# Attention in a decoder: transposes in half-array tiles, exponentials taken after the transpose, sums from the values' matmul

## The chip, the cores and the metric

The kernel runs on one core of a Trainium2 chip. The metric is the device time of one execution in microseconds, the median of several runs. The engines are TensorE (PE; its weight loads are shown apart as PEld), VectorE (DVE), ScalarE (ACT), GpSimd (POOL) and SyncE (SP), which issues the DMAs.

## The reference

A decoder of two layers on `x` of 8 batches, 256 tokens and 256 features, in float32, each sublayer followed by a residual addition and a layer norm:

```python
x = ln(x + gated_recurrence(x))                  # z = sigmoid, h by a scan over the tokens
x = ln(x + xattn0(x, ctx, bias, mask))           # 16 heads of 16, additive bias per batch
x = ln(x + ternary_ffn(ln'(x)))                  # activations quantised by one global maximum
x = ln(x + self_attn(x, rel_k, rel_v))           # distances clipped to 20 in scores and values
x = ln(x + xattn1(ctx, x, mask))
x = ln(x + gated_ffn(x))                         # 256 -> 768 -> 256, weights of int8 range

attn = softmax(q @ k.T / 4 + bias, axis=-1)      # 256 x 256 for each batch and head
out  = (attn @ v) @ Wo.T + bo
```

So there are 3 attentions x 8 batches = 24 items, each with 16 heads of 256x256 scores.

## The kernel before

**Order of the work.** Every piece of work is a Python generator that asks a planner (`Order`, L87) for an engine, a cost, the times at which its operands are ready, and buffers. The planner keeps a clock for each engine, takes the operation that can start first (among those within 0.1 us, the most urgent), and emits its instructions. So the order on each engine is fixed at build time by these costs; `either` and `copy` (L288) let it choose DVE or ACT for a copy. Tiles come from `Slots`, of which a task holds one until it drops it. There are 8 PSUM banks of 128x512 float32 (`banks`); `pv_left` lets two items at a time hold a bank for their values.

**Stages.** `recurrence` for 8 batches; `item_x0` (layer 0's cross-attention) for 8 batches; a barrier, since the quantisation needs a maximum over all batches; `quantised`; then `item_s1` (self-attention) and `item_x1` (layer 1's cross-attention) mixed by places set by hand (`S1_AT`, `X1_AT`); at the end `gated`, the last feed-forward. `keys_values` computes layer 1's keys and values into DRAM as filler. The self-attention sends its distance scores through DRAM scratch to skew them (`to_scratch`, `to_bands`, `tails_task`).

**One item.** `project_q`, `project_k` and `project_v` are each 8 TensorE passes of 256 columns. The 16 heads go as 4 quads of 4 heads (`quad`, L897):

- scores: 4 heads in 4 row tiles of 32 rows, each head into a bank of its own (L914);
- DVE takes each bank, adds the bias and writes the negated scores `sn` and their minimum `nm` (L942, a fused operation, 128x256 twice for each head);
- `head` (L953): ACT takes the exponential with `nm` as bias, and its sum over the keys (L958, 128x256 twice), into the quad's `p`;
- PE transposes the head's 256x256 by four 128x128 transposes into a bank (`transposed`, L503), and ACT or DVE copies it out to `pts` (L291, L292);
- `values` (L983): 4 heads in 4 column tiles of 32, into one bank that the item keeps through all four quads (L998).

`scales` (L1018) takes the reciprocals of the sums, POOL spreads them over the features (L1028), PE transposes them, they are copied to `oT`; `attend_out` multiplies the values by them (L1050), projects, adds the residual and norms. `norm` (L528) asks POOL for the root (L544, L549) and DVE for two scaled passes (L554). `distances` (L1454) adds the self-attention's distance values into the item's bank (L1483).

Weights for queries and keys come padded from DRAM (2 KB rows, L399) and POOL packs them (L477).

## Time and profile before

| | |
|---|---|
| median of 3 runs | 819.88 us (814.5 to 820.38) |
| span of the profiled execution, first to last instruction | 807.4 us |
| the median stands above this span by | 12.5 us |
| instructions | 21273 |
| granted TensorE clock, mean | 0.998 |
| DMA | 77.67 MB in 177681 packets, mean 96 GB/s |

The page gives the span of the profiled execution; what lies around it is read from the runs' median.

The engines' busy time in forty equal slices (tenths of a slice), with the DMA engines' mean busy share:

```profile
PE   7999999999999999997999999999999999999995
DVE  3998989989787698887799999898898999989986
ACT  2339999899988457786597799999999899845942
POOL 4440321122111044233333304313242323110010
DMA  5736352100100449889978706743656333100001
```

A slice is 20.2 us. The start and the last slice are thin; the dip of ACT and DVE near slices 13 to 15 is the barrier between the layers, and DMA is dense in slices 15 to 24, where the self-attention starts. A group's row gives its count, the busy time (overlaps counted once), the mean time of one instruction, and the idle time of its engine just before; neighbouring instructions overlap by some tenths of a microsecond, so the interval from start to start is shorter than the mean.

### The profile page before, as it was taken

The numbers are of one execution on the slowest core, as the hardware profiler recorded it, in microseconds if no ns is written. First come the engines' busy times: TensorE is split into PE (matmuls) and PEld (weight loads), VectorE is DVE, ScalarE is ACT, GpSimd is POOL, SyncE is SP. The second block draws the span as 40 slices with busy tenths as digits, with TensorE's granted clock in tenths as the row PEclk, the third lists the DMA queues.
The fourth block names the chain that finished last, engine by engine and source line by source line (L and its number), as shares of the span: only waits on it lengthen the run. The fifth ranks groups of instructions, "written<-read, shape, count | busy, mean of one in ns | idle before, by whom it ended". The sixth has DMA issues, their size and how long they took to land. (4 is left out here: it accounts for less than half of the span.)

```text
span 807.4 us, 21273 instructions
## 1 busy us (share of the span) xinstructions
PE 774.9 (96%) x7175; PEld 597.3 (74%) x7175; DVE 703.4 (87%) x2461; ACT 629.7 (78%) x2036; POOL 210.4 (26%) x398
## 2 busy tenths in 40 slices
PE   7999999999999999997999999999999999999995
PEld 6787777777766787665767677767776767899885
DVE  3998989989787698887799999898898999989986
ACT  2339999899988457786597799999999899845942
POOL 4440321122111044233333304313242323110010
PEclk9999999999999999999999999999999999999999
DMA  5736352100100449889978706743656333100001
GB/s 183 221 120 97 26 74 50 40 15 28 40 14 15 144 116 220 173 166 154 192 159 170 137 7 145 166 87 89 121 120 139 85 72 114 40 15 16 26 14 39
DMA packets 177681, 77.67 MB, mean 96 GB/s; under 512 B 155046, under 2 KB 171430, under 8 KB 177574
## 3 DMA queue, kind: packets, MB, share of 16 engines
q1 hardware_dynamic: 177574, 76.32, 43.4%
q8 instruction: 57, 0.93, 0.5%
q14 instruction: 50, 0.41, 0.2%
HBM read 41.66 MB, written 34.64 MB: 94 GB/s over the span
## 5 line engine op out<-in xcount | busy, mean ns | idle before, releaser
L958 ACT ACTIVATE p<-sn,nm 128x256 f32<-128x256 f32 x768 | 381.5, 510 | 14.1 <-DVE nm L942 8.2
L503 PE MATMUL pt<-ident,p 128*128 128x128 f32 x1536 | 208.4, 278 | 4.3 <-ACT p L958 1.8
L503 PEld LDWEIGHTS pt<-ident,p 128*128 128x128 f32 x1536 | 169.4, 141 | 50.5 <-ACT p L958 30.2
L292 ACT COPY pts<-pt 128x512 f32<-128x512 f32 x277 | 148.3, 591 | 34.5 <-PE pt L503 29.6
L958 ACT ACTIVATION_READ_ACCUMULATOR p<-sn,nm 128x1 f32 x768 | 154.4, 201 | 0.0
L914 PE MATMUL s<-k,q 32*128 32x256 f32 (+2 forms) x1792 | 118.6, 370 | 0.5 <-ACT pts L292 0.3
L998 PE MATMUL pv<-pts,v 128*32 128x256 f32 x1536 | 104.0, 385 | 0.0
L942 DVE CUSTOM_DVE_ANT_0 sn<-s,bias 128x256 f32<-128x256 f32 x256 | 93.1, 419 | 10.0 <-ACT p L958 5.8
L942 DVE CUSTOM_DVE_ANT_0 sn<-s,hide 128x256 f32<-128x256 f32 x256 | 92.8, 418 | 8.2 <-PE s L914 5.3
L942 DVE CUSTOM_DVE_ANT_0 sn<-s,band 128x256 f32<-128x256 f32 x256 | 92.3, 418 | 8.6 <-PE s L914 3.5
L914 PEld LDWEIGHTS s<-k,q 32*128 32x128 f32 x1792 | 77.2, 185 | 30.1 <-issue 20.1
L291 DVE COPY pts<-pt 128x512 f32<-128x512 f32 x107 | 71.1, 683 | 6.7 <-PE pt L503 6.3
L998 PEld LDWEIGHTS pv<-pts,v 128*32 128x32 f32 x1536 | 41.7, 109 | 41.5 <-issue 19.1
L942 DVE DVE_READ_ACCUMULATOR2_ANT nm<- 128x1 f32 x768 | 63.0, 82 | 0.0
L1028 POOL COPY rsw<-rsum 128x512 f32<-128x512 f32 x24 | 14.6, 610 | 157.4 <-DVE rsum L1022 139.0
L520 PE MATMUL pso<-wvo,oT 128*128 128x256 f32 x192 | 46.3, 385 | 0.4 <-ACT pts L292 0.4
L520 PEld LDWEIGHTS pso<-wvo,oT 128*128 128x128 f32 x192 | 35.1, 190 | 7.8 <-issue 1.3
L1354 POOL COPY band<-ends 64x256 f32<-64x256 f32 x64 | 21.5, 360 | 70.8 <-DVE nm L942 70.8
L1426 DVE TENSOR_REDUCE acc<-tail 128x8 f32<-128x864 f32 x32 | 33.4, 1045 | 5.3 <-POOL tail L1415 5.3
L1327 POOL COPY w<-w 128x504 f32<-128x504 f32 x32 | 19.6, 613 | 68.8 <-DVE w L291 40.7
L1709 ACT ACTIVATE sg<-fg 128x512 f32<-128x512 f32 x24 | 14.3, 599 | 21.7 <-PE fg L1698 21.6
L520 PE MATMUL psv<-wvo,ctxT 128*128 128x256 f32 x128 | 30.8, 384 | 0.0
(197 smaller groups left out, 1321.3 us busy)
## 6 DMA issues: line engine op xcount, KB each, us to landing
sk<-w SPq DMA_DIRECT2D x32, 416.0 KB
band<-sk SPq DMA_DIRECT2D x64, 104.0 KB
pb<-p SPq DMA_DIRECT2D x64, 104.0 KB
band<-sk SPq DMA_DIRECT2D x64, 84.0 KB
pb<-p SPq DMA_DIRECT2D x64, 84.0 KB
acc<-pb SPq DMA_DIRECT2D x32, 156.0 KB
ctxT<-in_ctxT SPq DMA_DIRECT2D x16, 256.0 KB
wpad<-in_qk_w SPq DMA_DIRECT2D x6, 512.0 KB
```

The lines of the kernel that those rows point to most:

```text
L291: ("DVE", on_dve(n), lambda: nc.vector.tensor_copy(dst, src)),
L292: ("ACT", on_act(n), lambda: nc.scalar.copy(dst, src)),
L503: nc.tensor.transpose(ps[:, c, t * P : (t + 1) * P], src[:, t, c * P : (c + 1) * P], ident)
L520: nc.tensor.matmul(ps[:, t, :], srcT[:, c, t * P : (t + 1) * P], w[:, c, :], start=(c == 0), stop=(c == KC - 1),)
L914: nc.tensor.matmul(ps[j].tile[:, t, first : first + w], it.q.tile[32 * j : 32 * j + 32, c, t * P : (t + 1) * P], k[32 * j : 32 * j + 32, c ...
L942: nc.vector.tensor_tensor_reduce(out=s.tile[:, t, :], in0=ps[j].tile[:, t, :], in1=tile[:, t, :], scale=-1.0, scalar=3e38, op0=ALU.add, op ...
L958: nc.scalar.activation(p.tile[:, j, q, :], s.tile[:, q, :], AF.Exp, bias=nm[:, q : q + 1], scale=-1.0, accum_out=it.sum_of(q, h),)
L998: nc.tensor.matmul(it.pv.tile[32 * j : 32 * j + 32, c, :], it.v.tile[:, k, head_of(n, j), :], pts.tile[:, k, :], start=(k == 0 and i == 0 ...
L1028: lambda: nc.gpsimd.tensor_copy(wide.tile.rearrange("p t (h d) -> p t h d", d=DH), rs.unsqueeze(3).to_broadcast([P, NQ, H, DH]),),
L1327: nc.gpsimd.tensor_copy(w.tile[:, :, NR:], w.tile[:, :, NR - 1 : NR].to_broadcast([P, HH, PBW - NR]))
L1354: nc.gpsimd.tensor_copy(band.tile[0:BLK, :, t, lo:hi], it.ends[c][0:BLK, t, i:HH:2].unsqueeze(2).to_broadcast([BLK, 4, hi - lo]),)
L1426: lambda: nc.vector.tensor_reduce(acc[:, c, :, own, 1], tail.tile, AX.X, ALU.add),
```

## The change

- Transposes (`transposed_pair`): two heads at a time, each 128x128 cut in two halves of 64 rows that are transposed in two row tiles of the array, into two banks; `pts` holds pairs (5 of them instead of 8 single ones).
- Cross-attention (`item.whole`, 16 of 24 items): no exponential before the transpose. DVE writes the negated, biased scores into `p`, POOL computes `nm - p` in place (`head_whole`), PE transposes, and ACT's exponential reads the transposed banks and writes `pts`. The sums come from the values' matmul: columns 16 to 31 of each head's values are ones. DVE's 32x32 block transposes, reciprocals and multiplications (`divided`) make `oT`. `scales` stays for the self-attention alone.
- Self-attention (8 items) keeps the exponential before the transpose; it has values tiles of its own, and its distances go into a bank of their own and are added by DVE.
- Values: a bank for each quad (cross) or two quads (self) instead of one for the item.
- The fourth bank of each quad's scores is copied to `p` by ACT, and DVE's minimum then reads `p`. The `sn` buffers are gone; the quad's `p` is taken together with the score banks.
- Query and key weights are loaded packed, in pieces of 64 bytes; POOL's packing is gone.
- Fewer buffers: one `oT`; one `y`, one `v`, one `mask8` and one `hide` (bfloat16) for layer 1's cross-attention; the mask of layer 0 shares `neg`. The planner may skip a starved task when nothing else can go, has other costs for changes of tile shape, and gives 0.5 us for a pair's transposes.

```diff
+    def transposed_pair(ps, srcs):
+        for j, src in enumerate(srcs):
+            for c in range(2):
+                for t in range(2):
+                    for g in range(2):
+                        own = slice(g * BLK, (g + 1) * BLK)
+                        nc.tensor.transpose(
+                            ps[g][:, 4 * j + 2 * c + t, :],
+                            src[own, t, c * P : (c + 1) * P],
+                            ident[own, own],
+                            tile_position=(g * BLK, 0),
+                        )
...
+    def minimum(it, n, j, p, ps, t_s, tile, t_b, t_bias, left, times):
+        own = p.tile[:, j]
...
+        if j != 3:
+            t = yield from do("DVE", 0.7, [t], lambda: least(ps.tile))
+            ps.drop(t)
+        else:
+            t = yield from do("ACT", on_act(512), [t_s], move)
+            ps.drop(t)
+            t = yield from do("DVE", 0.7, [t, t_b, t_bias], lambda: least(own))
...
+    def head_whole(it, n, j, p, nm, t, left):
+        def emit():
+            for q in range(NQ):
+                own, m = p.tile[:, j, q, :], nm[:, q : q + 1]
+                nc.gpsimd.tensor_scalar(own, own, -1.0, m, ALU.mult, ALU.add)
+        t = yield from do("POOL", 0.9, [t], emit)
...
+    def pair(it, n, m, done):
+        ps = [Held(banks, f"pt{it.name}_{n}_{m}_{g}") for g in range(2)]
...
+        for g in range(2):
+            dst = halves_of(pts.tile)[g]
+            if it.whole:
+                t = yield from do(
+                    "ACT", on_act(512), [t_p, pts.at],
+                    lambda: nc.scalar.activation(dst, parts(g), AF.Exp),
+                )
+            else:
+                t = yield from copy([t_p, pts.at], dst, parts(g))
...
-            it.token = yield from get(pv_left, "")
-            it.pv = Held(banks, f"pv{it.name}")
+        if it.whole or i == 0:
+            pv = it.pv[n] = Held(banks, f"pv{it.name}_{n}")
+        else:
+            pv = it.pv[n - 1]
...
+    def divided(it, c, i, pv, t):
...
+            lambda: nc.vector.transpose(
+                u[:, :, i : i + 2, :].rearrange("p n a d -> p n (a d)"),
+                pv.tile[:, 0, :].rearrange("p (n e) -> p n e", e=32),
+            ),
...
+            nc.vector.reciprocal(rec, u[:, :, i + 1, 0])
+            nc.vector.tensor_tensor(
+                u[:, :, i, :], u[:, :, i, :], rec.unsqueeze(2).to_broadcast([P, n, DH]), ALU.mult
+            )
...
+            lambda: nc.vector.transpose(
+                it.oT.tile.rearrange("p c (n e) -> p (c n) e", e=32),
+                it.u.tile[:, :, 0:2, :].rearrange("p n a d -> p n (a d)"),
+            ),
...
-    mask8_bufs = slots(work, "mask8", 2, [P, NQ, S], U8)
-    hide_bufs = slots(work, "hide", 2, [P, NQ, S])
+    mask8_bufs = slots(work, "mask8", 1, [P, NQ, S], U8)
+    hide_bufs = slots(work, "hide", 1, [P, NQ, S], BF16)
```

## The prediction

> **What bounds the kernel now.** First I read the engines' busy time on the profile's page, then the same in five stretches cut where the stages change.

> ```profile
> PE 774.9 (96%) x7175; PEld 597.3 (74%) x7175; DVE 703.4 (87%) x2461; ACT 629.7 (78%) x2036; POOL 210.4 (26%) x398
> ```
> ```profile
> 0.00:94.00 94.00, 87.92 (x593) 71.58 (x594) 75.81 (x241) 50.79 (x155) 32.00 (x56) 1.00 0.57 139
> 94.00:271.00 177.00, 173.59 (x1562) 129.19 (x1560) 150.29 (x584) 153.80 (x522) 31.31 (x43) 1.00 0.16 38
> 271.00:400.00 129.00, 119.97 (x1029) 89.28 (x1030) 109.50 (x349) 88.23 (x258) 44.54 (x104) 1.00 0.84 169
> 400.00:692.00 292.00, 288.30 (x3067) 212.20 (x3068) 268.80 (x1033) 271.47 (x933) 88.97 (x172) 1.00 0.55 116
> 692.00:807.40 115.40, 105.09 (x931) 95.00 (x929) 99.00 (x258) 65.37 (x173) 13.62 (x25) 0.99 0.06 19
> ```

> Columns: stretch, length, busy us of PE, weight loads, DVE, ACT, POOL; then granted clock, DMA share, GB/s. From 94 to 271 us layer 0's cross-attention runs alone (seven items, 25.3 us each); 271 to 400 is the barrier and the filling of layer 1, with DMA at 0.84; 400 to 692 is self- and cross-attention mixed; then the last feed-forward. PE's busy time has modelled ends, so I price PE by the starts in its timeline:

> ```profile
> 548.98 1.19 PE L914 MATMUL s<-k,q 32*128 32x148 f32 x24
> 550.10 2.00 PE L520 MATMUL pso<-wvo,oT 128*128 128x256 f32 x8
> 551.93 1.89 PE L509 MATMUL psq<-xT_l1a,wqk 128*128 128x256 f32 x8
> 553.65 2.35 PE L503 MATMUL pt<-ident,p 128*128 128x128 f32 x20
> 555.93 0.50 PE L914 MATMUL s<-k,q 32*128 32x256 f32 x4
> ```

> A projection (8 of 256 columns) takes 551.93 to 553.65: 1.72 us, 0.215 each. A 128x128 transpose takes 2.28/20 = 0.114 (0.109 inside a burst). Four tiles of 32 rows run at once: 24 score matmuls in 1.12 us; a whole quad's 16 take about 0.86, its 16 values matmuls 0.88. One layer 0 item therefore costs PE 4 x (0.86 + 1.75 + 0.88) for its quads, 4 x 1.73 for projections, 2 x 0.44 for other transposes, some 22 with tile changes: 22 of 25.3 us. The other engines' prices:

> ```profile
> L958 ACT ACTIVATE p<-sn,nm 128x256 f32<-128x256 f32 x768 | 381.5, 510 | 14.1 <-DVE nm L942 8.2
> L503 PE MATMUL pt<-ident,p 128*128 128x128 f32 x1536 | 208.4, 278 | 4.3 <-ACT p L958 1.8
> L292 ACT COPY pts<-pt 128x512 f32<-128x512 f32 x277 | 148.3, 591 | 34.5 <-PE pt L503 29.6
> L942 DVE CUSTOM_DVE_ANT_0 sn<-s,bias 128x256 f32<-128x256 f32 x256 | 93.1, 419 | 10.0 <-ACT p L958 5.8
> L291 DVE COPY pts<-pt 128x512 f32<-128x512 f32 x107 | 71.1, 683 | 6.7 <-PE pt L503 6.3
> ```

> From start to start (neighbours overlap) an exponential with its sum takes 0.49 us, ACT's copy 0.477, a DVE minimum 0.345, DVE's copy 0.60. ACT then spends 32 x 0.49 + 11.5 x 0.477 = 21.2 us on an item, DVE about 20.6 (11.0 on minima). So three engines are within 10% of each other and each loses some 12% to the others. No chain through one engine explains the time; relieving one leaves the next.

> **The change part by part.**

> *Transposes in row tiles.* 1536 of 128 columns become 3072 of 64 columns, in two halves of the array. By 0.109/128 a 64-column one streams 0.055. If the halves run together, a pair of heads costs 8 x 0.055 = 0.44, against 0.87: 0.43 x 192 pairs = 83 us off PE. The gain's lower bound is zero: 16 x 0.055 = 0.88. I take 0.46, nearest the score rows, where four 32-row tiles overlap; with about 70 more changes of tile shape (410 against 343 in program order) at 0.09 (a score-to-transpose step is 0.305 against 0.216), PE falls by some 73 us, 3.3 per item.

> [...] The score rows above, 24 loads of 32x128 inside 1.12 us, show that loads into different rows overlap.

> *Late exponentials.* In 16 of 24 items the 512 row exponentials of 0.49 go; 256 of 128x512 from PSUM replace both them and the copies out. Their price lies between ACT's copy (0.477) and twice a 256-wide one (0.98); a 512-wide tanh from PSUM starts 0.488 before its successor, the same shape, so 0.49. Per item ACT goes from 21.2 to 16 x 0.49 + 4 x 0.477 (the fourth score bank) = 9.8, some 11 with copies moved there; over the kernel about 614 to 465.

> *POOL's multiply-and-add.* 512 of 128x256. The row of 128x512 (mean 748, 0.617 when undisturbed) bounds one above by 0.62; 128x2 at 0.19 bounds it below. 64x256 copies start 0.34 apart; I take 0.36 to 0.40, between 512 and 2 elements. An item's POOL work goes from 4.3 to about 16 us, less than the pace, but 200 us in all, and the norms' root, the bias addition and the residual addition now queue behind it.

> *Sums out of the values, division on DVE.* Per x item: four transposes of 128x256 (0.33 as other 256-wide rows, up to 0.60 if at half rate), four reciprocals (0.15) and multiplications of 128 elements (0.2), one transpose of 128x512 (0.6): 3.3 us. Gone: 4.5 copies of 0.60, the scale's copy, reciprocal and product (1.3), a few projections' outputs that the planner now gives to ACT (0.5). Net about -1.1 per item. Self-attention keeps its exponentials and gains two additions and copies of 256: about level. Over the kernel DVE loses some 27 of 676 us. That is little: DVE is the engine left.

> *What POOL takes from DVE.* DVE's normalising pass, SBUF to SBUF, is normally 0.41 us:

> ```profile
> L554 DVE TENSOR_SCALAR xn<-xb,mv_l0x,rs_l0x x16: 401/408/1358, 93.7 to 270.7; 128x256 f32<-128x256 f32 x16
> ```

> Its one 1358 lies beside a 1.27 us POOL addition; a two-SBUF-input g<-g,h went from 0.68 to 0.93 beside POOL, and an a<-z on POOL to 1657. Minima on PSUM are 0.42 either way. The fourth minimum now reads two SBUF operands (192 of them), so with the norms and divisions about 17 DVE instructions an item can meet POOL. Free: 0. Each waiting for a whole POOL instruction: 17 x 0.36 = 6 us. POOL is busy 50 to 70%, and half an instruction is left on average: 17 x 0.6 x 0.18 = 1.8 per item.

> [...]

> *Buffers.* Values no longer keep two of eight banks for an item's length, and the fourth bank leaves early: worth the few per cent that PE loses on waits, at most. A quad's scores now also wait for one of three p buffers, each held over minima, POOL and transposes, some 9 us: one every 3 us, against a pace of 5.7, so nothing. Against the gain, layer 1's cross items have one mask, one values and one output buffer instead of two. A drain between them costs 0 (feed-forward work covers it) to 6 us (a quad's chain); if the cover is gone, twice in the last stretch. I put 2 us there.

> *Queues.* SP issues the six weight loads as twelve, 0.47 us each, and no unpacking on POOL (0.75 x 6) follows. 64-byte pieces: the nearest 80-byte packets take 12 ns, so 4096/16 x 12 = 3.1 us per weight against 256/16 x 84 = 1.3: +11 us of transfer in a start where recurrences on DVE (24 of 25 us busy from 25 to 50) cover it; bare, the two first weights would cost 3.6. Masks share a buffer with what they become; the wait is behind an addition 20 us earlier.

> *Sum by stretch.* 0 to 94: 0. 94 to 271: PE 18.5 to 19, DVE 19.5 + 1.8 = 21.3; with the other two relieved, DVE can run at 0.93, its share in the best stretch (47.9 of 50 busy from 400 to 450, less overlap): 22.9 an item, 7 x 2.4 = -17. 271 to 400: DMA holds, -4. 400 to 692: DVE 268.8, less 12 moved or removed, plus about 11 of waits, 267.5; at 0.97 busy 276: -16. 692 on: 2.7 items of 3.3 us less on PE, half of it on the path as DVE is level there, -5, and the drain +2: -3. Together -40: span 807.4 to 767.4. The median of the runs, 819.88, stands 12.5 above that span, and I carry it: **780 us**.

> **The rivals.**
> 1. Balance comes freely: the waits on POOL's side do not matter and all stretches run at today's share of their greatest work (0.88). PE 635 and DVE 650 of a span 650/0.88 = 739 plus 12.5: 752. For it: ACT's relief and the freed banks; against it DMA at 0.84 from 271 to 400.
> 2. The halves do not overlap in the array (the change does not do what it says): PE stays at 712 plus 6 for tile changes, and only ACT's relief remains: 718/0.91 + 12.5 = 802. Against it: the score rows.
> 3. POOL becomes the bound, and the time ends above today's. An item holds 4 + 32 x POOL's price; it reaches 25.3 x 0.95 at 0.62 us each, the undisturbed price of twice the elements. At 0.83, the a<-z mean among DVE work, it is 30.6/0.95 = 32 us an item: 7 x 6.9 = +48 in the first attention stretch, -20 elsewhere: 807 + 28 + 12.5 = 848.

> **How the numbers follow.** Forecast 0.58 (780; its own range 766 to 802: half or twice the waits on POOL, -12 and +24 us over the two attention stretches, less what the buffers return), rival 1 0.17, rival 2 0.13, rival 3 0.12. Leaving out the far part of rival 3 and the lower half of rival 1 gives 745 to 822. A measurement of this kernel can tell about 1% from no change, 812 to 828: faster takes the forecast, rival 1 and 0.05 of rival 2, 0.80; same the other 0.08 of rival 2 and 0.01 of rival 3, 0.09; slower the rest of rival 3, 0.11.

> **What would show it.** Right: pt bursts of 16 in about 0.46 us; ACT below 500 us busy and idle in the first attention stretch; DVE the busiest engine over 90%; POOL near 400; minima that read p longer than those that read s. Wrong: pt starts 55 ns apart singly (rival 2); POOL rows above 0.6 with transposes waiting for POOL (rival 3); DVE below 85% with PE full (rival 1, or a stall that I missed). A reciprocal or transpose on DVE at twice my price would add some 20 us to DVE and put the time near 797.

## The result, and the profile after

The changed kernel takes 826.9 us (median of 15 runs, 820.7 to 830.5), the kernel before 819.6 in the runs beside it: a ratio of 1.0075, 95% interval 1.005 to 1.010. The profiled execution spans 820.5 us (before: 807.4). The forecast was 780 us, with 745 to 822 as its range: wrong in sign, and outside. The time lies in the band from 812 to 828 that the prediction called no change, to which it gave 0.09.

The profile before shows an execution that is shorter than the others. The 74 executions of that kernel that were timed beside the experiments span 813.2 to 822.3 us (median 816.7), and their times stand only 1.7 to 3.0 us above their spans. So most of the 12.5 us between the median and the profiled span is not something that lies around the span. The 15 executions of the changed kernel span 825.2 us in the median. In these two profiles the kernels differ by 13 us, in the medians of their times by 7.

The engines' busy time of the changed kernel, then the same in the five stretches of the prediction (columns as there):

```profile
PE 755.2 (92%) x8647; PEld 557.1 (68%) x8647; DVE 706.1 (86%) x2528; ACT 494.8 (60%) x1233; POOL 472.7 (58%) x888
```
```profile
0.00:94.00 94.00, 84.66 (x547) 65.11 (x548) 67.43 (x198) 29.42 (x61) 43.66 (x79) 0.96 0.53 106
94.00:271.00 177.00, 171.67 (x2127) 124.15 (x2124) 161.09 (x661) 99.10 (x196) 147.53 (x263) 1.00 0.27 55
271.00:400.00 129.00, 115.67 (x1169) 80.66 (x1168) 105.94 (x345) 93.51 (x270) 47.15 (x104) 0.96 0.81 158
400.00:692.00 292.00, 270.79 (x3707) 190.53 (x3703) 264.57 (x1024) 220.28 (x615) 187.41 (x356) 0.98 0.61 116
692.00:820.50 128.50, 112.45 (x1108) 96.62 (x1106) 107.06 (x305) 52.48 (x96) 47.00 (x88) 0.97 0.05 18
```

ScalarE lost 135 us, as intended, and POOL gained 262. VectorE did not get lighter (703 to 706), and TensorE only by 20 of the 73 us forecast. New is the third column from the right, the granted clock: 1.00 or 0.99 in every stretch before, now 0.96 to 0.98 in four of the five. In forty slices of the page:

```profile
PE   7999999999999888989898999999899998999985
DVE  3898798999997797877887899998999997899984
POOL 2446798998984253333345749466575786223630
PEclk9998999999999999989999999999999999999997
```

POOL is over 80% busy in most of slices 6 to 12 (layer 0's cross-attention), and TensorE, which was at 9 nearly everywhere, has gaps in slices 14 to 22, and in 29 and 34. Where the time went, by the starts of single instructions in the two timelines:

| us from the span's start | before | after | forecast of the step | measured |
|---|---|---|---|---|
| first x after layer 0's cross-attention | 94 | 112 | 0 | +18 |
| eighth of them (seven items) | 271 | 269 | -17 | -20 |
| second x after self-attention | 396 | 397 | -4 | +3 |
| eighth of them | 678 | 676 | -16 | -3 |
| end of the span | 807.4 | 820.5 | -3 | +15 |

So the pace of layer 0's items came as forecast (25.3 to 22.4 us, forecast 22.9), and a late start took it back. From 400 us on nothing was gained: self-attention ends at the same time, and the cross items mixed with it are behind (the fifth of them ends at 660 us, before at 646). The last stretch lost the rest: the sixth ends at 694 us (before 692), the seventh at 760 (734), the eighth at 797 (778).

One more number orders all that follows. The planner in the kernel keeps a clock of its own while the kernel is built. It ends at 795 us for the kernel before and at 772 us for the changed one. The traces are 12 and 48 us longer than these plans. By its own plan the change was worth 23 us, not 40; and the chip ran 36 us further behind the new plan than behind the old (by the median spans 21.5 and 53.1 us behind, so 31.6 further). Most experiments below ask why.

### The profile page after: what moved, and what is told of

Read it like the earlier page. It is cut to its first block, busy times and chain, and to the rows that moved or that the text cites. A ratio compares the mean times of both kernels' runs of the same rounds, so it can differ in the third digit from the quotient of the medians.

```text
span 820.5 us, 23679 instructions
## 1 busy us (share of the span) xinstructions
PE 755.2 (92%) x8647; PEld 557.1 (68%) x8647; DVE 706.1 (86%) x2528; ACT 494.8 (60%) x1233; POOL 472.7 (58%) x888
## 4 chain that ended last, share of the span: by engine, by line
DVE 23%; PE 19%; POOL 7%; ACT 7%; DMA 7%; issue 3%; SPq 1%; POOLq 0%; DVEq 0%; ACTq 0%
DVE p L991 7%; POOL p L1021 5%; PE s L962 3%; ACT p L1061 3%; PE pt L529 3%; PE pv L1094 3%; DMA sk<-w 3%; PE pso L554 2%; DVE sg L1868 1%; DMA band<-sk 1%; DVE sg L1875 1%; PE psa L1605 1%; DMA acc<-pb 1%; DVE acc L1561 1%; PE psq L543 1%
## 5 line engine op out<-in xcount | busy, mean ns | idle before, releaser
L1021 POOL TENSOR_SCALAR p<-p,nm 128x256 f32<-128x256 f32 x512 | 269.7, 544 | 43.7 <-DVE nm L991 37.4
L529 PEld LDWEIGHTS pt<-ident,p 64*128 64x128 f32 x3072 | 116.5, 141 | 69.9 <-POOL p L1021 27.7
L1046 ACT ACTIVATE pts<-pt 128x512 f32<-128x512 f32 x256 | 135.0, 605 | 45.0 <-PE pt L529 43.3
L529 PE MATMUL pt<-ident,p 64*128 64x64 f32 x3072 | 144.1, 233 | 19.2 <-ACT p L1061 4.8
L1061 ACT ACTIVATE p<-p,nm 128x256 f32<-128x256 f32 x256 | 127.5, 507 | 4.0 <-DVE nm L991 3.9
L997 ACT COPY p<-s 128x512 f32<-128x512 f32 x96 | 56.4, 588 | 64.7 <-PE s L962 57.6
L991 DVE CUSTOM_DVE_ANT_0 p<-s,band 128x256 f32<-128x256 f32 x192 | 69.7, 415 | 5.3 <-PE s L962 3.1
L991 DVE CUSTOM_DVE_ANT_0 p<-s,hide 128x256 f32<-128x256 f32 x192 | 69.1, 414 | 5.9 <-PE s L962 5.8
L991 DVE CUSTOM_DVE_ANT_0 p<-s,bias 128x256 f32<-128x256 f32 x192 | 69.3, 411 | 1.8 <-PE s L962 1.6
L312 ACT COPY pts<-pt 128x512 f32<-128x512 f32 x88 | 47.0, 586 | 5.6 <-PE pt L529 5.4
L554 PE MATMUL pso<-wvo,oT 128*128 128x256 f32 x192 | 47.6, 391 | 2.4 <-DVE oT L1159 1.4
L554 PEld LDWEIGHTS pso<-wvo,oT 128*128 128x128 f32 x192 | 34.6, 189 | 11.4 <-ACT p L997 1.5
```

The costliest lines, as they stand in the source:

```text
L312: ("ACT", on_act(n), lambda: nc.scalar.copy(dst, src)),
L529: nc.tensor.transpose(ps[g][:, 4 * j + 2 * c + t, :], src[own, t, c * P : (c + 1) * P], ident[own, own], tile_position=(g * BLK, 0),)
L554: nc.tensor.matmul(ps[:, t, :], srcT[:, c, t * P : (t + 1) * P], w[:, c, :], start=(c == 0), stop=(c == KC - 1),)
L991: nc.vector.tensor_tensor_reduce(out=own[:, t, :], in0=src[:, t, :], in1=tile[:, t, :], scale=-1.0, scalar=3e38, op0=ALU.add, op1=ALU.min, ...
L997: nc.scalar.copy(own, ps.tile)
L1021: nc.gpsimd.tensor_scalar(own, own, -1.0, m, ALU.mult, ALU.add)
```

## The experiments

Three of them keep every engine's order of instructions as in the changed kernel (`fill`, `fill_thin`, `nosub_kept`; `bank4_fill` keeps that of `bank4`). In the others the planner arranges the whole program anew, and that alone moves the time: a second mask buffer moved the plan's end by 10 us. So I give the plan's end beside each span. Spans are those of the profiled execution. "Half clock" is the time in it with a granted clock of 0.5, without the last piece at the end of the program.

| kernel | plan's end | span | behind plan | half clock, us | ratio to before, 95% interval |
|---|---|---|---|---|---|
| before | 795 | 807 | 12 | 0 | 1 |
| changed | 772 | 820 | 48 | 31 | 1.0075 (1.005 to 1.010) |
| fill | 772 | 816 | 44 | 10 | 1.0016 (0.999 to 1.004) |
| fill_thin | 772 | 821 | 49 | 27 | 1.0057 (1.004 to 1.008) |
| nosub_kept | 772 | 813 | 41 | 34 | 0.991 (0.988 to 0.994) |
| nosub | 768 | 814 | 46 | 34 | 0.990 (0.985 to 0.994) |
| beside | 764 | 828 | 63 | 48 | 1.016 (1.012 to 1.021) |
| act4 | 780 | 826 | 46 | 55 | 1.010 (1.006 to 1.013) |
| bank4 | 783 | 814 | 31 | 34 | 0.999 (0.997 to 1.001) |
| two_banks | 785 | 866 | 81 | 55 | 1.062 (1.057 to 1.066) |
| nosub_bank4 | 782 | 833 | 51 | 51 | 1.020 (1.016 to 1.024) |
| bank4_fill | 783 | 818 | 35 | 24 | 1.003 (1.000 to 1.005) |
| rowt_before | 806 | 836 | 30 | 41 | 1.020 (1.016 to 1.024) |
| fullt | 817 | 860 | 43 | 24 | 1.050 (1.047 to 1.053) |
| early | 822 | 883 | 61 | 85 | 1.077 (1.074 to 1.081) |
| packed | 778 | 839 | 61 | 55 | 1.025 (1.021 to 1.029) |
| packed_bank4 | 781 | 824 | 43 | 44 | 1.002 (0.999 to 1.005) |
| selfact | 784 | 838 | 55 | 58 | 1.022 (1.018 to 1.026) |
| hide2 | 782 | 833 | 51 | 48 | 1.019 (1.017 to 1.021) |
| costs | 796 | 830 | 34 | 27 | 1.020 (1.016 to 1.024) |

### First round: the start, POOL, VectorE

My first theories were that the late start and POOL made the loss, with VectorE as the bound after 400 us. Four kernels tested them.

**packed**: the padded weight loads and POOL's packing put back.

```diff
-                for c in range(KC):
-                    events["wqk", o] = yield from dma(...  # 64-byte pieces
+                packed = yield from get(p_bufs, f"wpad{o}")
...
+                order.spawn(50 + o, compact(o, packed, t, w, ready))
```

> The changed kernel with the six query and key weights loaded padded again (2 KB rows) and packed by POOL, as before. If the strided loads on SP's queue made the late start: the first scores move from 69.9 us back to some 57, layer 0's attention (its last x rows at 269 us) ends 10 to 15 us earlier, and the time falls from 826.9 to some 812 to 817. Rival, the start is covered later on (the stretch after 271 us waits for DMA, or the planner's order simply differs): the first scores move, and the time stays within 4 us of 826.9. Rival, the start is late for another reason (PE or DVE order of the recurrences): the first scores stay near 70 us.

Measured: 841.7 us, slower, though the start did come earlier: first scores at 64.6 us instead of 69.9, first x at 104 instead of 112. SP's queue in the changed kernel shows what the strided loads cost (columns: start, duration, what was issued):

```profile
31.99 5.14 SPq L422 DMA_DIRECT2D wqk<-in_qk_w  x2
...
38.94 2.75 SPq L422 DMA_DIRECT2D wqk<-in_qk_w  x2
...
43.66 2.80 SPq L422 DMA_DIRECT2D wqk<-in_qk_w  x2
...
48.27 3.46 SPq L422 DMA_DIRECT2D wqk<-in_qk_w  x2
...
53.82 0.43 SPq L1266 DMA_DIRECT2D ctxT<-in_ctxT  x1
```

The six pairs take 2.5 to 5.1 us of SP, where I had counted 0.47 for each load. The first load of a pair takes 0.55 to 0.67 us; the second takes 1.9 to 4.5, and the plain `wvo` load behind it 1.2 to 1.5 (in the kernel before 0.37 to 0.56, once 1.1). So the context that opens the attention is issued at 53.8 us (before: 34.3). None of the times expected came, so something was missing from my list of causes. The mean granted clock gave the hint: 0.962 here, 0.976 in the changed kernel, 0.998 before.

**nosub** and **beside**: POOL's subtraction left out (in both, the subtraction of the row maximum is missing); in `beside` POOL does the same work on a tile that nobody else uses, and nobody waits for it.

```diff
-        t = yield from do("POOL", 0.9, [t], emit)      # nosub: no such step
...
-                    lambda: nc.scalar.activation(dst, parts(g), AF.Exp),
+                    lambda: nc.scalar.activation(dst, parts(g), AF.Exp, scale=-1.0),
```

> The changed kernel without POOL's subtraction in the cross-attention: the transposes wait for DVE's minimum alone, and the exponential takes scale -1 and no row maximum (the kernel leaves out the subtraction of the maximum). If POOL sets the pace or its latency costs: layer 0's items go from 22.4 to some 20 us, the last stretch loses 6 to 10 us, and the time falls to some 785 to 800. If only what POOL takes from DVE matters: rows of DVE that read SBUF go from 501 to some 415 ns at the least, and the time falls as far as in the run where POOL works beside, or not. Rival, DVE holds the pace anyhow at 0.91 of its time: 815 to 825.

> [...] If the wait for POOL costs: the time is near that of the run without subtraction, 790 to 800. If contention for SBUF, or POOL's queue ahead of the norms' roots, costs: the time is near the changed kernel's 826.9, 815 or more.

Measured: 812.1 and 834.6 us. Taking the wait for POOL away while POOL still works gains nothing; taking the work away gains 1.8%. It points to POOL's work in itself and not to the wait, but plan and half clock differ (48 us in `beside`), so `nosub_kept` below repeats it in a fixed order.

**selfact**: the self-attention's copies out of PSUM all on ScalarE.

```diff
-                t = yield from copy([t_p, pts.at], dst, parts(g))
+                t = yield from do("ACT", on_act(512), [t_p, pts.at], lambda: nc.scalar.copy(dst, parts(g)))
```

> The changed kernel with all 64 copies of the self-attention's transposes out of PSUM on ScalarE (some 40 of them were on DVE at about 0.6 us). If DVE bounds 400 to 692 us: DVE's busy time there falls by some 20 us from 264.6, ACT's rises from 220 to some 240, and the time falls by 8 to 20 us, to 807 to 819. Rival, PE at 0.93 with its changes of tiles and the chains through the buffers bound it: within 5 us of 826.9.

Measured: 839.9 us, outside both expectations. VectorE fell to 695 us busy and the time rose by 13: VectorE's load alone does not set the end. Half-clock time is 58 us.

### TensorE's clock

This is what I had missed. TensorE of the changed kernel in its timeline (start, duration; the idle time before it and what ended it in brackets):

```profile
429.30 0.71 PE L1452 MATMUL psr<-drel,q 128*128 128x328 f32 x2
432.86 1.02 PE L1605 MATMUL psa<-ident,acc 128*82 128x128 f32 x4 [2.85 <-DMA acc<-pb]
433.81 2.09 PE L962 MATMUL s<-k,q 32*128 32x256 f32 x16
435.83 0.85 PE L1605 MATMUL psa<-ident,acc 128*82 128x128 f32 x4
```

TensorE waits 2.85 us for a transfer, and then 16 score products take 2.02 us to the next start, where they took 1.08 before. The stretches around this gap and two others show the clock (third column from the right):

```profile
74.50:78.00 3.50, 2.33 (x42) 1.63 (x34) 3.50 (x21) 1.96 (x4) 3.50 (x8) 0.99 0.30 60
78.00:81.00 3.00, 2.80 (x28) 1.75 (x32) 2.46 (x16) 1.78 (x4) 3.00 (x6) 0.50 0.21 43
...
429.00:432.50 3.50, 1.01 (x5) 0.44 (x3) 3.50 (x16) 2.41 (x10) 1.09 (x2) 1.00 1.27 142
432.50:436.00 3.50, 3.14 (x21) 1.97 (x22) 0.69 (x2) 0.58 (x1) 0.00 (x0) 0.56 1.45 133
675.00:678.50 3.50, 1.26 (x26) 0.96 (x22) 3.22 (x10) 2.31 (x5) 3.33 (x6) 1.00 0.02 5
678.50:682.00 3.50, 3.50 (x45) 2.06 (x43) 2.66 (x13) 0.89 (x2) 3.41 (x7) 0.52 0.64 225
```

Each time some 3.5 us in which TensorE does little (2.33, 1.01 and 1.26 us busy) are followed by half clock. In the profiled execution of the kernel before no such piece stands ahead of the end. That execution's mean granted clock, 0.998, is matched by 2 of the 74 others: they lie between 0.988 and 0.998, with a median of 0.992, so most of them lose a little of the clock too. The 15 executions of the changed kernel lie between 0.964 and 0.983, with a median of 0.972.

**fill** puts work into such gaps, and **fill_thin** is its control: the same places and about the same time, but a sixteenth of the array. Apart from the fillers every engine's order is the changed kernel's.

```diff
+            if engine == "PE":          # ahead of 25 operations, 101 fillers in all
+                self.warm(held.tile, FILL.get(self.at_pe, 0))
...
+    def warm(bank, count):
+        for _ in range(count):
+            nc.tensor.transpose(bank[:, 0, 0:P], ident, ident)                              # fill
+            nc.tensor.matmul(bank[0:32, 0, 0:64], ident[0:32, 0:32], ident[0:32, 0:64], ...)  # fill_thin
```

> The changed kernel, the order of every engine kept instruction for instruction, with 101 additional 128x128 transposes of the identity (0.109 us each) into banks that the next operation overwrites, put ahead of 25 operations before which TensorE stood idle in the changed kernel's trace. Theory of the clock: the granted clock falls to half when the array is little used over a window of 3.4 us (nine such windows, 30.7 us, in the changed kernel outside its last stretch of 10 us, none before the last matmuls in the kernel before), and each microsecond at half clock costs up to half a microsecond; with the gaps filled the time at half clock falls below 15 us and the time from 826.9 to some 815 to 822. Rival, the clock follows the waits and costs nothing, because other engines hold the pace: the time at half clock falls, and the time stays at 825 to 832 (the fillers cost up to 11 us where a gap has moved).

> The control of the run with fillers: the same 101 fillers ahead of the same 25 operations, but products of a 32x32 piece of the identity (two passes of 64 columns, about as long as the transpose of 128 that they replace), which use a sixteenth of the array. Theory of the clock (the gate counts how much of the array is used): the half-clock time stays near the changed kernel's 30.7 us, 24 or more, and the ratio near its 1.0075, 1.005 to 1.012. Rival (any instruction in the gap keeps the clock up, or the fillers help by their place): half-clock time under 15 us, and 0.999 to 1.004 as with the full fillers.

Measured: 820.7 and 823.3 us, ratios 1.0016 and 1.0057; half clock 10 and 27 us. The place above in `fill`:

```profile
425.67 1.91 PE L290 MATMUL psa<-ident 128*128 128x128 f32 x16
427.89 0.61 PE L1620 MATMUL psa<-ident,acc 128*82 128x128 f32 x4 [0.32 <-DMA acc<-pb]
428.43 1.15 PE L977 MATMUL s<-k,q 32*128 32x256 f32 x16
429.51 0.64 PE L1620 MATMUL psa<-ident,acc 128*82 128x128 f32 x4
```

The fillers end 0.32 us before the transfer does, and the scores take 1.08 us again. The thin fillers left the half clock where it was, and most of the time. So what the fillers won back is 0.4 to 0.6% of the time (the spans of the two differ by 4.9 us), most of the difference from the kernel before; and between these two runs the clock went with how much of the array the fillers use (half clock 10 us with all of it, 27 with a sixteenth, 31 without fillers), not with whether TensorE executes something. It is a small part of the 47 us that the forecast missed.

The clock's whole price may be higher. `fill` still has 10 us at half clock, and among the 15 executions of the changed kernel the time rises as the clock falls, from 820.7 us at 0.983 to 830.5 at 0.964 (correlation 0.96, 0.3 us for each microsecond at half clock). Whether the lost clock makes these executions longer, or a longer wait costs the clock, they do not tell.

**rowt_before**: row tiles alone, put into the kernel before.

```diff
-        t = yield from do("PE", TURNS, [t_e, ps], lambda: transposed(ps.tile, p.tile[:, j]))
+            lambda: transposed_pair([parts(g) for g in range(2)], srcs), "t",   # two heads, two banks
```

> The kernel before with nothing but the transposes in row tiles, two heads at a time (and the copies out by pairs of banks). The prediction's step: TensorE 73 us less busy, and since ScalarE and VectorE are within 10 per cent of it, a gain of 5 to 15 us (805 to 815). Theory of the clock: TensorE now waits, and windows at half clock appear (over 10 us in all) where the kernel before had none; the gain is lost, 815 to 830. If the row tiles do not run together: TensorE stays as busy, 820 to 830, without half-clock windows.

```profile
PE 770.6 (92%) x8711; PEld 569.7 (68%) x8711; DVE 703.2 (84%) x2462; ACT 629.5 (75%) x2037; POOL 209.0 (25%) x396
```

Measured: 837.4 us, 2% slower than without them and above every expected range. The plan is 11 us longer already (probably because a pair needs two heads and two banks at once), the half clock is 41 us, as the theory of the clock had it, and VectorE and ScalarE have the same work as before, in more time: TensorE's relief had nowhere to go.

### POOL and the fourth bank

**nosub_kept**: as `nosub`, but the planner believes that POOL's step is there, so that all else keeps its order.

```diff
             for q in range(NQ):
-                own, m = p.tile[:, j, q, :], nm[:, q : q + 1]
-                nc.gpsimd.tensor_scalar(own, own, -1.0, m, ALU.mult, ALU.add)
+                pass
```

> The changed kernel without POOL's subtraction (the kernel leaves out the subtraction of the row maximum), the planner believing that it is still there, so that every engine's order is the changed kernel's with POOL's 512 instructions gone. If POOL (its latency before the transposes, and its meeting with VectorE in SBUF) is what holds the run behind its plan: the span falls behind the plan's 772 by less than 28 us instead of 48, VectorE's busy time falls by 15 us or more, and the ratio is 0.970 to 0.985. Rival, the clock and VectorE's own prices are: 0.995 to 1.005.

```profile
PE 749.1 (92%) x8647; PEld 556.6 (68%) x8647; DVE 690.8 (85%) x2528; ACT 493.7 (61%) x1233; POOL 203.2 (25%) x376
```

Measured: 813.0 us, ratio 0.991. Between the two theories: POOL's pass costs 1.6%, some 13 us, with VectorE's same 2528 instructions 15 us shorter. The rest of the distance to the plan, 41 us, is not this pass's.

What VectorE loses to POOL shows in the minima, of which those of three heads in four read PSUM (`s`) and one in four reads SBUF (`p`). Changed kernel (minimum, median and longest in ns):

```profile
L991 DVE CUSTOM_DVE_ANT_0 p<-s,bias x192: 377/414/425, 71.9 to 251.8; 128x256 f32<-128x256 f32 x192
...
L991 DVE CUSTOM_DVE_ANT_0 p<-p,bias x64: 373/415/809, 73.9 to 252.9; 128x256 f32<-128x256 f32 x64
```

In `nosub_kept`, where POOL doesn't pass over `p`:

```profile
L991 DVE CUSTOM_DVE_ANT_0 p<-p,bias x64: 377/419/425, 73.7 to 244.4; 128x256 f32<-128x256 f32 x64
```

From PSUM none of the 192 in the changed kernel is over 0.43 us, though 185 of them overlap a POOL instruction in time. The 64 from SBUF all overlap one; 24 of them are over 0.43, up to 0.81.

**bank4** takes the copy of the fourth bank away (all minima read PSUM), **two_banks** copies two.

```diff
-        if j != 3:
+        if True:       # bank4; two_banks: if j < 2:
             t = yield from do("DVE", 0.7, [t], lambda: least(ps.tile))
```

> The changed kernel with the fourth bank's minimum read by VectorE from PSUM as the other three (no copy on ScalarE, 96 of 0.48 us, and no minimum that reads two operands in SBUF). If the minima on SBUF lose time to POOL: VectorE's busy time falls by 5 to 10 us and the time to 815 to 822. If the early release of the fourth bank is what it is worth: scores wait longer for banks, and the time is 832 or more. By the prediction (a few per cent of TensorE at most) no change beyond 1 per cent.

> The suspected cost doubled: the changed kernel with two of each quad's four score banks copied out by ScalarE and their minima read in SBUF, instead of one (none of them: 817.4 us, ratio 0.999; one: 826.9, 1.0075). If minima on two SBUF operands and POOL's passes hold each other up: POOL's busy time rises from 473 by another 30 us, VectorE's from 706 by 15 to 20, and the ratio goes to 1.015 to 1.025. Rival, the gain without the copy was a luck of the order: busy times rise by less than 5 us (POOL) and the ratio is anywhere.

Measured: 817.4 and 868.6 us; ratios 0.999, 1.0075 and 1.062 for none, one and two banks, and 31, 48 and 81 us behind the plan. Busy times of `bank4`, then of `two_banks`:

```profile
PE 751.3 (92%) x8647; PEld 557.8 (69%) x8647; DVE 687.2 (84%) x2522; ACT 447.3 (55%) x1143; POOL 439.2 (54%) x888
```
```profile
PE 773.6 (89%) x8647; PEld 566.0 (65%) x8647; DVE 734.6 (85%) x2550; ACT 530.5 (61%) x1306; POOL 499.8 (58%) x887
```

POOL is busy 34 us less without the copies and 27 more with twice as many. The durations of the 512 passes alone sum to 249, 278 and 304 us for none, one and two banks. VectorE goes with them; without the copies it fell by 19 us, where I had expected 5 to 10. With two, single minima take up to 1.49 us:

```profile
L991 DVE CUSTOM_DVE_ANT_0 p<-p,bias x128: 375/418/1487, 73.0 to 268.2; 128x256 f32<-128x256 f32 x128
```

The loss grew faster than I expected (1.015 to 1.025).

**nosub_bank4**: both edits at once, to see whether the copy also costs where POOL is idle.

> The changed kernel without the copy of the fourth bank and without POOL's subtraction (the kernel leaves out the subtraction of the row maximum, as in the earlier run). If the meeting of POOL and VectorE in SBUF explains the gain of 0.8 per cent without the copy, that gain is already had where POOL is idle: the time is that of the run without the subtraction, 0.985 to 0.995 (808 to 815). Rival, the copy costs by itself (ScalarE's queue ahead of the minimum): 0.975 to 0.984.

Measured: 834.7 us, outside both expectations: with POOL idle, giving the copy up loses 3% (0.990 to 1.020), so the bank's early release may then be worth something. But this kernel is also slower than `bank4` with all of POOL's work in it, which no price explains; 51 us at half clock and another order may be part of it. Differences of 2% between re-planned kernels are not proof of anything by themselves here. What stands on the copy is its direction over none, one and two banks together with the busy times and the rows above.

**act4**: one head in four has its multiply-and-add on ScalarE.

```diff
+        if j == 3:
+            t = yield from do("ACT", 2 * on_act(256), [t], emit)   # Identity, scale -1, bias m
```

> The changed kernel with the multiply-and-add of one head in four on ScalarE (Identity, scale -1, the row's minimum as bias) instead of POOL. POOL's busy time falls by some 65 us, ScalarE's rises by some 60. If POOL bounds the cross-attention or its latency holds the banks: layer 0's items go below 22 us and the time falls to 805 to 818. Rival, it is the order and the array's clock: 822 to 840.

Measured: 823.6 us; POOL fell by 63 us, ScalarE rose by 38, and layer 0's items took 23.1 us (22.4 in the changed kernel). No gain that can be told apart, with 55 us at half clock.

**bank4_fill**: fillers in `bank4`, order kept.

> The changed kernel without the copy of the fourth bank, every engine's order as in that run, with 90 transposes of the identity of 0.109 us ahead of 15 operations before which TensorE stood idle in that run's trace (34 us at half clock there, outside the last 6). The clock's theory: time at half clock below 17 us, and a ratio of 0.990 to 0.996 against 0.9992, so that this version beats both kernels. Rival: the clock costs nothing where VectorE holds the pace, 0.997 to 1.003.

Measured: 820.5 us, no gain. Half clock fell only from 34 to 24 us; 23 of the fillers run at 790 and 795 us, where the last chain runs, and the last norms come 4 us later than without them. Fillers placed by one trace do not carry far, and the version that I hoped for does not beat the kernel before. No kernel here that computes everything did; `bank4` equals it.

### The parts taken back, and the rest

**fullt**: 128x128 transposes again. **early**: the cross-attention's exponentials ahead of the transposes again, no pass on POOL.

```diff
-            lambda: transposed_pair([parts(g) for g in range(2)], srcs), "t",
+            lambda: [transposed(ps[g].tile, srcs[g]) for g in range(2)],        # fullt
...
-                nc.gpsimd.tensor_scalar(own, own, -1.0, m, ALU.mult, ALU.add)
+                nc.scalar.activation(own, own, AF.Exp, bias=m, scale=-1.0)      # early
```

> The changed kernel with each head's 128x128 transposes as before (1536 of 0.109 us) instead of the 3072 in row tiles. By the prediction's price this puts 70 to 83 us back on TensorE. If TensorE were the bound: 860 or more. Theory of the clock: the transposes in row tiles use half the array for the same time as half of them would use all of it, so undoing them raises the array's use and the time at half clock falls from 30.7 us to under 12 us; with the other engines holding the pace the time stays within 10 us of 826.9 (817 to 837).

> The changed kernel with the cross-attention's exponentials ahead of the transposes again (on ScalarE, in place, without sums, which still come from the values' matmul), and the copies out by VectorE or ScalarE; POOL's multiply-and-add is gone. ScalarE goes from 495 to some 610 us busy, VectorE up by some 30 from copies. If POOL's work costs more than it saves: 815 to 825, faster than the changed kernel. If the late exponentials are worth what the prediction said: 840 or more.

Measured: 861.5 and 883.8 us. Both parts do work inside the changed kernel: without the row tiles it is 4% slower, without the late exponentials 7%. In `fullt` TensorE is busy 39 us more and the span is 40 us longer, as its first expectation had it (860 or more), so inside the changed kernel TensorE's relief does reach the end; the half clock is 24 us and not under 12. In `early` POOL's pass does not cost more than it saves, which was the first of my two expectations: VectorE, which has the divisions of the new scheme and now the copies as well, goes to 776 us. The late exponentials pay for the divisions; together they leave VectorE where it was.

**packed_bank4**: the early start again, with the fourth copy gone.

> The changed kernel without the copy of the fourth bank and with the padded weight loads of the kernel before. If the start (first x after layer 0's attention at 107 us, 94 in the kernel before) is a loss that lasts: that x comes at 98 or earlier and the ratio falls from 0.999 to 0.985 to 0.992. Rival, recurrences that run first are work done early, which the attention then doesn't have to share: ratio 0.996 to 1.01.

Measured: 820.5 us, ratio 1.002; the first x comes at 100 us instead of 107, the eighth at 263 instead of 262. The late start is not a loss that lasts: in the changed kernel all eight recurrences are done by 90 us, ahead of the first item's x (in the kernel before the eighth ends at 154 us, among the items), and the attention then has the engines to itself.

**hide2**: two mask buffers in layer 1.

```diff
-    hide_bufs = slots(work, "hide", 1, [P, NQ, S], BF16)
+    hide_bufs = slots(work, "hide", 2, [P, NQ, S], BF16)
```

> The changed kernel with two mask buffers in bfloat16 for layer 1's cross-attention instead of one, so that an item's mask can be made while the item before still reads its own. If the single buffers lengthened the last stretch: the two last cross items overlap more, and the time falls by 4 to 10 us, 817 to 823. Rival, values and outputs are single too, and the order moves anyhow: 825 to 840.

Measured: 833.1 us, slower. In the changed kernel the last cross item's query projection starts at 754 us, just after the output projection of the one before (753); in the kernel before they overlapped (692 and 728). With two mask buffers the two start at 757 and 762 us, 5 us apart. So the mask alone is not what serialises them; the single values, `u` and `y` buffers are left, and two of each were not tried.

**costs**: the planner's prices for POOL's pass and the divisions set to the trace's.

```diff
-        t = yield from do("POOL", 0.9, [t], emit)
+        t = yield from do("POOL", 1.1, [t], emit)
...
-        t = yield from do("DVE", 0.35, [t], emit)
+        t = yield from do("DVE", 0.5, [t], emit)
```

> The changed kernel with three of the planner's prices raised to what the changed kernel's trace shows: 1.1 us instead of 0.9 for a head's two multiply-and-adds on POOL, 0.40 instead of 0.34 for a block transpose on VectorE, 0.5 instead of 0.35 for a reciprocal with its multiplication. The instructions are the same, their order is not. By the planner's own clock the changed kernel would end at 772 us and this one at 796, the kernel before at 795; the traces ran 48, and 12 for the kernel before, behind the plan. Theory of the prices: the gain that the order was made for rests on prices that POOL and VectorE do not hold, so with true ones the run is behind its plan by 30 or less and takes about what it took, 815 to 832. Rival, the wrong order is itself the loss: with true prices the time falls below 810. Rival, other things than these prices hold the run behind: it is 40 or more behind this plan too, 840 or more.

Measured: 832.7 us, 34 behind a plan of 796, just outside the first expectation (30, and 832 at most). With true prices the planner itself sees no gain over the kernel before (795), and the run is nearer to its plan. The better-informed order is not a faster one.

## Why the prediction was wrong, step by step

- **What bounds the kernel.** "Relieving one leaves the next" was right, and I then did not hold to it. Taking 53 us off the transposes (190 to 137 us from start to start) and 135 off ScalarE left VectorE and the waits between engines, and the time with them. TensorE's own price was low as well: counted to the next operation, a quad's scores took 1.08 us in the kernel before and its values 1.00, not 0.86 and 0.88.
- **Row tiles: right in kind, too large in size.** A pair's 16 starts span 0.49 us, forecast 0.46, with 16 weight loads of 0.139 us each (median) among them, so the halves and their weight loads run together and rival 2 is out. But to the next operation it is 0.64 us, and the step took 53 us off TensorE (idle time left out), not 73. Of these, TensorE's busy time shows only 20: its bursts now wait inside, a quad's scores from 1.08 to 1.30 us in the median.
- **Late exponentials: right.** ScalarE went down by 135 us of a forecast 149, an exponential from PSUM starts 0.478 after the last.
- **POOL's pass: mis-sized.** 0.46 us from start to start undisturbed, 0.54 in the mean, against 0.36 to 0.40. The rows:

```profile
L1021 POOL TENSOR_SCALAR p<-p,nm 128x256 f32<-128x256 f32 x512 | 269.7, 544 | 43.7 <-DVE nm L991 37.4
L529 PEld LDWEIGHTS pt<-ident,p 64*128 64x128 f32 x3072 | 116.5, 141 | 69.9 <-POOL p L1021 27.7
L1046 ACT ACTIVATE pts<-pt 128x512 f32<-128x512 f32 x256 | 135.0, 605 | 45.0 <-PE pt L529 43.3
```

  TensorE's weight loads now wait 28 us for POOL. That is rival 3 in part: POOL is near its limit in layer 0 but does not set the pace, 22.4 us against 25.3 before; the whole pass is worth 1.6%, by `nosub_kept`. The price of 0.83 us that rival 3 puts on a pass is the mean of the five `a<-z` that overlap VectorE's work (four at 0.62, one at 1.66); the mean of all eight is 0.748.
- **VectorE: mis-sized.** A division costs 3.8 us an item by the medians from start to start (23.5 + 14.4 + 13.4 + 10.1 us over 16 items), forecast 3.3, and 40 copies stayed on VectorE in the self-attention. Undisturbed its work fell by 12 us, not 27; POOL took 15 back.
- **Queues: wrong, and without lasting effect.** Strided loads held SP for 2.5 to 5.1 us a pair instead of 0.94; the start is 18 us late; `packed_bank4` shows that bringing it forward gains nothing.
- **The sum, step "400 to 692": the step that failed.** I let VectorE go "at 0.97 busy 276". It stayed at 0.91 (264.6 of 292 us; before 268.8), and the stretch gave nothing. The chain of work that ended last shows what took TensorE's place. From 518 to 692 us, in the kernel before and in the changed one (shares of the stretch):

```profile
by line: PE pt L503 21.6%; ACT p L958 12.7%; PE s L914 12.0%; PE pv L998 12.0%; PE pso L520 7.4%; PE psq L509 5.1%; DVE sn L942 4.8%; ACT pts L292 4.5%; PE psa L1468 3.9%; issue 3.2%; PE psk L509 2.0%; PE ps_rs L503 1.6%; PE pv L1483 1.5%; 
```
```profile
by line: POOL p L1021 19.3%; DVE p L991 14.7%; PE pv L1094 5.0%; PE s L962 4.9%; PE pt L529 4.6%; DVE acc L1561 4.5%; PE pso L554 4.5%; issue 4.3%; DMA sk<-w 2.8%; DMA acc<-pb 2.6%; DMA kin<-xk 2.2%; DVE hide L1758 2.0%; DVE xb L1205 1.8%; 
```

  Before, the chain is TensorE and ScalarE; now POOL's pass and VectorE's minima lead it, and the transfers are in it. Leading the chain is not yet the bound: without the pass the time falls by 1.6%. Over the whole program the relief on two engines turned into waits, on TensorE above all, whose idle time (span less busy) grew from 32 to 65 us. Busy shares of one stretch are no promise that another will reach them when an engine beside is relieved.
- **Not in the forecast at all: the clock.** I read 1.00 or 0.99 in each row of the profile before and took it as given. The profiled execution has no window of 3.41 us with less than 0.40 of the array in use; in the other traces 129 of 148 windows below 0.35 were followed by half clock (last section). Fillers won back 0.4 to 0.6%.
- **Buffers and the last step, "692 on": +2 us forecast in a step of -3.** From the last self-attention to the end it is 15 us more, a miss of 18. The sixth cross item ends 3 us later than before, the seventh 25: the last two run one after another. How much each of the single buffers bears stays open.
- **The 12.5 us on top.** Most of them were the distance of one short execution from the median; in the changed kernel the median stands 6.4 us above the profiled span.

Of the 36 us by which the changed kernel runs further behind its plan in the profiles, the runs in fixed order show 8 for POOL's pass and 4 for the fillers, by their profiled spans. By the median spans (before 816.7 us, changed 825.2, `nosub_kept` 811.3, `fill` 819.0) it is 13.9 and 6.2 of 31.6. The fourth bank's copy is inside the first of these as far as it meets POOL. The rest, some 11 us if the two add up, which no run shows, stays unassigned. That it is many small waits in an order without slack is how I read the timeline; it was not shown.

## What to carry to other kernels

Before counting a relief on one engine as time, ask which engine would have to get busier for it, and take that engine's present share as the limit. Where the order of work is fixed by a planner's prices, compare its planned end with the trace for both versions: no kernel here came out as well against the kernel before as its plan did, and what a new operation costs beyond its price in the plan, or takes from another engine, comes on top. Before reading a small difference off two profiles, see where each profiled execution lies among the timed ones. And when TensorE is made lighter, check whether its granted clock stays (here 0.992 before and 0.972 after, medians of the executions).
